# Cross-attention with layer norm on one core: the order of all engines' work written anew, with sums left in PSUM, copies moved between engines and low parts last

## The chip, the cores and the metric

The kernel runs on one core of one Trainium2 chip. The metric is the device time of one execution in microseconds (us). TensorE does the matrix products, VectorE and ScalarE work on SBUF and PSUM, GpSimd on SBUF, and SyncE starts most transfers. In the profile they are called PE (with PEld for the loads of weights), DVE, ACT, POOL and SP.

## The reference

```
qs  = (x @ wq)   per head (16 heads of 32), x: 4 x 2048 x 512, float32
ks, vs = (ctx @ wk), (ctx @ wv) per head, ctx: 4 x 77 x 512
scores = einsum('bhqd,bhkd->bhqk', qs, ks) / sqrt(32)
scores = where(mask, -inf, scores)
attn   = softmax(scores) @ vs
out    = attn @ wo + x
return (out - mean(out)) / sqrt(var(out) + 1e-5) * gamma + beta
```

## The kernel before

The 8192 rows of x are 64 tiles of 128 rows. Tiles t = 0 to 63 go in pairs (b = t // 2) and in groups of four (g = t // 4). To keep float32 accuracy, a large matrix is split into a high part and a low part (what the high part lost), both read by TensorE at full rate, and a product is high x high + high x low + low x high: 12 matmuls of 512 columns for 4 chunks c of the contraction.

A word of the table `ORDER` is one step; the first letter says what, the number which tile, pair or group. Each engine executes its own steps in the order of the table, and waits for the others through semaphores. The steps that matter here:

- `Qk` (L275, q_rows; 12 large matmuls into one PSUM bank, pq) makes a quarter of the queries of a group, `qk` (L289) copies it from PSUM to SBUF on VectorE. `i` and `j` (L265 on ScalarE, L269 on GpSimd) make the high part xth and the low part xtl of x.
- `St` (L405; 64 small matmuls into four banks, sc) makes a tile's scores. `Tt.part` (L422, VectorE) adds the mask, moves them to SBUF (pbuf) and takes the maxima of four heads, `et.part` (L437, ScalarE) the exponentials of four heads, `r` (L447, VectorE) the reciprocals of the sums, `n` (L452, GpSimd) the normalisation, `t` (L473, VectorE) a transpose, `Pb.n` (L484) one of twelve transfers that regroup a pair's transposed tiles into PT; the letter behind the number is the issuing queue (s SyncE, a ScalarE, g GpSimd).
- `Vb` (L498; 32 small matmuls into two banks, pa) multiplies a pair's PT with the values. `ab.i` (L527, ScalarE) takes the high part AH out of PSUM, `bb.i` (L531, VectorE) the low part AL.
- `Ot` (L554, o_proj; 12 large matmuls into one bank, po) is the output product of a tile. `+t` (L563, VectorE) adds the rows of x and writes the sum to SBUF (o), which frees the bank. `st` (L577, L578, VectorE) takes mean and variance, `vb` (L583 to L586, four small GpSimd steps) the factor and the shift of a pair (rn), `kt` (L592, ScalarE) scales, `ft` and `)t` (L595, L598, GpSimd) apply gamma and beta, `wt` (L601) stores.
- The last eight tiles, 56 to 63, go another way: `&` (L566) adds in PSUM, `s` or `~` takes the moments from PSUM, `u` (L618, L619, GpSimd) makes the factor, `y` and `z` (L634, L637, VectorE) finish.

There are eight PSUM banks; the table SLOTS["mm"] says which bank each product gets. A product can begin when the step that empties its bank's last user is done.

227 steps of the table stand on TensorE. Between two kinds of step (large, scores, values) TensorE changes the shape of its matmuls.

Of the kernel before, what the change touches and what calls it, by code (L numbers as in the profile page):

```python
# [8 lines left out]
F32 = mybir.dt.float32  # L9
# [25 lines left out]
for b in range(4):  # L35
# [7 lines left out]
NPB = 3  # L43
KSCALE = 1.0 / HD**0.5
# [30 lines left out]
T22.0 +12 T22.3 k10 k11 r20 n20 T22.2 T22.1 P9.0s O13 +13 P9.7s P9.11s e22.0 g17 s13 e21.2 e22.1 e21.0 P9.8s Z12.s
e21.3 P9.3s s12 v6 j15 b7.1 e22.2 Q26 x14 q26 t20 Q27 q27 r21 n21 S23 T23.3 T23.0 T23.1 g16 P9.1s e22.3 r22 V8 a8.1
b8.1 k13 e23.0 x15 a8.0 f4 t21 e23.3 e23.1 T23.2 e23.2 S24 T24.2 e24.2 T24.1 )4 b8.0 Q29 i17 n22 T24.3 f10 i16 )10 q29
T24.0 t22 f13 )13 e24.0 O14 +14 r23 e24.1 s14 S25 T25.0 T25.3 e25.3 n23 j16 T25.1 x16 O16 +16 e25.1 O15 +15 t23 s15 v7
O17 S26 T26.3 j17 e24.3 k15 T26.0 T25.2 P10.8s P10.4s r24 n24 V9 P10.7s P10.2s T26.1 k14 P10.0s w10 P10.6s P10.5s w13
P10.9s x17 P10.11s w4 +17 P10.1s P10.10s a9.1 b9.1 P10.3s e26.3 P11.5s s17 a9.0 e25.2 e25.0 T26.2 P11.3s P11.8s P11.7s  # L80
P11.1s P11.4s s16 v8 e26.0 k17 b9.0 f15 x19 P11.10s P11.2s Q28 q28 Q31 q31 g18 r25 n25 t24 P11.11s k12 g19 f17 k16 f16
)15 Q30 e26.1 q30 S27 T27.2 T27.3 T27.1 e27.2 V10 T27.0 e27.0 x18 e26.2 a10.1 t25 S28 T28.1 T28.2 f11 )11 r26 n26
P11.6s T28.0 P11.0s )17 P11.9s T28.3 w15 O19 +19 a10.0 b10.0 t26 P12.8s P12.0s P12.9s P12.3s w11 Q33 e27.3 P12.2s
P12.5s e28.1 e27.1 r27 f14 n27 b10.1 i19 i18 P12.7s O18 +18 s18 S29 T29.0 s19 v9 e28.2 w17 V11 a11.1 a11.0 T29.3 e28.3
b11.0 x23 P12.10s e28.0 k18 j18 t27 P12.4s x20 T29.2 e29.2 P12.1s O20 +20 O21 P13.8s P12.11s P13.5s P13.1s P12.6s
T29.1 P13.3s e29.1 e29.3 )14 w14 P13.2s s20 S30 j19 )16 T30.1 b11.1 T30.0 r28 n28 T30.3 e29.0 r29 e30.1 e30.0 k19
# [12 lines left out]
P17.0s f26 Q41 q41 n37 e38.2 P17.10s P17.8s P17.4s k27 w23 x31 k28 Q42 q42 S39 T39.2 P17.5s w25 T39.1 T39.3 e38.3 f27
k29 i24 P17.11s V16 a16.0 t37 j24 e39.3 r38 b16.0 n38 x30 P17.3s P17.9s S40 T40.3 T40.1 T39.0 e40.3 e39.1 P18.10s  # L100
P18.11s P18.8s P18.3s x32 P18.2s )26 P18.1s P18.6s P18.9s x33 O30 +30 s30 T40.0 O31 +31 t38 Q47 T40.2 a16.1 e39.0
e39.2 r39 n39 f28 s31 v15 b16.1 e40.2 e40.0 f29 )29 )28 S41 T41.3 e40.1 e41.3 T41.2 t39 V17 g25 T41.0 a17.1 T41.1
e41.2 L3 P18.4s P18.7s Q45 r40 w26 P18.5s b17.1 P18.0s P19.6s g27 n40 w28 P19.8s q47 Q44 q44 k31 f31 k30 f30 a17.0 i25
j25 S42 T42.1 P19.0s P19.1s P19.7s O33 e41.1 e41.0 )27 T42.0 T42.2 T42.3 e42.3 b17.0 O32 r41 +33 e42.0 s33 t40 S43 +32
e42.2 P19.9s P19.10s T43.2 P19.3s x34 w29 T43.0 P19.11s P19.2s T43.3 g26 x35 P19.5s P19.4s e42.1 T43.1 r42 n41 n42 s32
v16 t41 e43.3 V18 a18.0 a18.1 Q46 Q50 )31 =48.8 e43.1 e43.0 q46 q45 P20.5s i27 j27 P20.3s S44 P20.1s P20.9s x38 w27
q50 b18.0 P20.10s P20.7s T44.1 T44.0 x37 w31 T44.2 t42 O34 k33 T44.3 f33 e43.2 i26 k32 e44.0 e44.1 S45 T45.0 r43
# [67 lines left out]
def xattn_layernorm(  # L175
# [84 lines left out]
    def load_xT(g, c):  # L260
        fx[g, c] = buf([P, 2, GRP], F32, "xtf", name=f"xtf_{g}_{c}")
        nc.sync.dma_start(fx[g, c], xT[g, :, c : c + 2])
# [538 lines left out]
```

## Time and profile before

| what | value |
|---|---|
| time, median of 3 runs | 508.02 us (506.6, 508.02, 508.16) |
| span of the profiled execution, first to last instruction | 506.2 us |
| mean granted clock of TensorE | 0.998 |
| busy: PE, DVE, ACT, POOL | 498.8, 460.5, 473.9, 421.3 us |
| HBM read, written | 41.79 MB, 16.78 MB |

The profiled execution's own time is not listed apart from its span; the runs lie 0.4 to 2.0 us over it, for what is around the first and the last instruction. A group's row gives line, engine, operation, output and inputs, shape, count, busy time in us, the mean of one in ns, and the idle time ahead of it with what ended it. A timeline's row gives start, duration and the same names. In the busy line, PE counts matmuls whose ends are modelled and which overlap; the distance between two starts is what one costs.

### The profile page before, as it was taken

Reading aid. Unit: us, or ns where it says so; the run is one execution under the profiler, and the core shown is the slowest. Engines: PE = TensorE matmul, PEld = TensorE weight load, DVE = VectorE, ACT = ScalarE, POOL = GpSimd, SP = SyncE. Lnnn points to the kernel's source line nnn. Section 1 sums busy time; section 2 is a strip of 40 time slices with the busy share of each in tenths; the row PEclk is TensorE's granted clock in tenths of the full one; section 3 lists DMA queues with packets and bytes.
Section 4 is the critical chain, followed back from the end, with each engine's and each line's share of the span. In section 5 each row is a group of like instructions: output and inputs, shape, how many; then the busy total and the mean of one; then the engine's idle time right before and its main releaser. Section 6 shows DMA issues by size and latency. Waiting matters only on the chain.

```text
span 506.2 us, 20312 instructions
## 1 busy us (share of the span) xinstructions
PE 498.8 (99%) x6831; PEld 383.1 (76%) x6831; DVE 460.5 (91%) x2539; ACT 473.9 (94%) x2248; POOL 421.3 (83%) x387
## 2 busy tenths in 40 slices
PE   9999999999999999999999999999999999999995
PEld 6987778777777777777777777777777777877773
DVE  5799988999899999898898898998999999899997
ACT  6699999999999999999999999999999998999851
POOL 2666464789886798989989887999998999999896
PEclk9999999999999999999999999999999999999999
DMA  8957577889886796859887778877888769888746
GB/s 306 396 197 175 135 212 183 221 210 217 247 242 178 177 248 199 249 165 253 243 216 204 200 207 240 230 201 193 248 232 225 207 177 293 247 199 222 183 150 232
DMA packets 58782, 110.86 MB, mean 219 GB/s; under 512 B 9462, under 2 KB 11278, under 8 KB 58678
## 3 DMA queue, kind: packets, MB, share of 16 engines
q1 hardware_dynamic: 54502, 101.30, 71.1%
q0 software_dynamic: 2496, 5.77, 4.0%
q10 hardware_dynamic: 1680, 2.49, 2.0%
q8 instruction: 54, 0.88, 0.8%
q14 instruction: 50, 0.41, 0.3%
HBM read 41.79 MB, written 16.78 MB: 116 GB/s over the span
## 4 chain that ended last, share of the span: by engine, by line
PE 98%; DMA 1%; DVE 1%; ACT 0%; issue 0%; DVEq 0%
PE po L554 36%; PE pq L275 35%; PE pa L498 11%; PE sc L405 11%; PE pv L326 2%; PE pk L299 1%; PE pq L685 1%; DMA stage_a<-kin 1%; PE pa L513 0%; DVE xtl L637 0%; PE po L543 0%; DVE st L606 0%; DVE po L634 0%; ACT woh L672 0%; DVE mvt L608 0%
## 5 line engine op out<-in xcount | busy, mean ns | idle before, releaser
L437 ACT ACTIVATE pbuf<-pbuf,nm 128x77 f32<-128x77 f32 x1024 | 353.0, 358 | 5.2 <-DVE nm L422 3.6
L437 ACT ACTIVATION_READ_ACCUMULATOR pbuf<-pbuf,nm 128x1 f32 x1024 | 203.2, 198 | 0.0
L422 DVE CUSTOM_DVE_ANT_0 pbuf<-sc,mb 128x77 f32<-128x77 f32 x1024 | 169.7, 231 | 7.4 <-PE sc L405 5.8
L452 POOL TENSOR_TENSOR pbuf<-pbuf,ri 128x1232 f32<-128x1232 f32 x63 | 142.2, 2258 | 36.7 <-DVE ri L447 25.4
L554 PE MATMUL po<-woh,AH 128*128 128x512 f32 x256 | 103.5, 404 | 0.0
L473 DVE STREAM_TRANSPOSE B<-pbuf 128x1280 f32<-128x1280 f32 x64 | 96.1, 1502 | 5.8 <-POOL pbuf L452 2.4
L275 PE MATMUL pq<-xth,wqh 128*128 128x512 f32 (+1 forms) x256 | 100.8, 394 | 0.2
L554 PE MATMUL po<-wol,AH 128*128 128x512 f32 x256 | 99.9, 390 | 0.0
L554 PE MATMUL po<-woh,AL 128*128 128x512 f32 x256 | 99.8, 390 | 0.0
L275 PE MATMUL pq<-xth,wql 128*128 128x512 f32 (+1 forms) x256 | 98.1, 383 | 0.0
L275 PE MATMUL pq<-xtl,wqh 128*128 128x512 f32 (+1 forms) x256 | 98.1, 383 | 0.0
L422 DVE DVE_READ_ACCUMULATOR2_ANT nm<- 128x1 f32 x1024 | 84.4, 82 | 0.0
L598 POOL TENSOR_TENSOR o<-o,bet 128x512 f32<-128x512 f32 x56 | 72.1, 1291 | 1.8
L595 POOL TENSOR_TENSOR o<-o,gam 128x512 f32<-128x512 f32 x56 | 72.2, 1293 | 0.1
L269 POOL TENSOR_TENSOR xtl<-xtf,xth 128x1024 fp32r<-128x1024 f32 x28 | 67.2, 2404 | 3.9 <-ACT xth L265 3.2
L405 PEld LDWEIGHTS sc<-kct,q 32*64 32x64 f32 x4096 | 51.4, 130 | 22.6 <-issue 12.2
L405 PE MATMUL sc<-kct,q 32*64 32x77 f32 x4096 | 61.2, 238 | 0.0
L498 PE MATMUL pa<-PT,vsb 96*32 96x256 f32 x992 | 59.7, 382 | 0.0
L554 PEld LDWEIGHTS po<-woh,AH 128*128 128x128 f32 x256 | 48.0, 188 | 14.3 <-issue 2.5
L275 PEld LDWEIGHTS pq<-xth,wqh 128*128 128x128 f32 x256 | 48.1, 188 | 13.7 <-DVE nm L422 1.2
L554 PEld LDWEIGHTS po<-woh,AL 128*128 128x128 f32 x256 | 48.1, 188 | 10.5 <-DVE AL L531 0.2
L275 PEld LDWEIGHTS pq<-xth,wql 128*128 128x128 f32 x256 | 48.1, 188 | 9.7
(108 smaller groups left out, 638.6 us busy)
## 6 DMA issues: line engine op xcount, KB each, us to landing
PT<-B SPq DMA_DIRECT2D x330, 128.0 KB
xtf<-xT SPq DMA_DIRECT2D x28, 512.0 KB
o<-x SPq DMA_DIRECT2D x56, 256.0 KB
out<-o SPq DMA_DIRECT2D x56, 256.0 KB
PT<-B POOLq DMA_DIRECT2D x25, 128.0 KB, 4.0
PT<-B ACTq DMA_DIRECT2D x17, 128.0 KB
stage_a<-kin SPq DMA_DIRECT2D x4, 410.0 KB
xtf<-xT SPq DMA_DIRECT2D x4, 256.0 KB
```

Source lines behind the costliest of these rows:

```text
L269: return nc.gpsimd.tensor_tensor(l[:, c : c + 2], fx.pop((g, c)), xh[g][:, c : c + 2].bitcast(F32), ALU.subtract)
L275: nc.tensor.matmul(pq, w[:, c, m * P : (m + 1) * P], r[g][:, c, rs], start=(n == 0), stop=(n == 11))
L326: nc.tensor.matmul(pv[: rows.stop - rows.start], ctx_s[c][i][:, rows], v[c], start=(n == 0), stop=(n == 11))
L405: mm = nc.tensor.matmul(sc[j][r0 : r0 + SR, g * NK : (g + 1) * NK], qs[q, g, rs.start + r0 : rs.start + r0 + SR], kct[q, g, t // TPB, keys ...
L422: nc.vector.tensor_tensor_reduce(pb[:, h // 2, (h % 2) * NK : (h % 2 + 1) * NK], scs[t][j][:, g * NK : (g + 1) * NK], mb[:, t % TPB, keys_ ...
L437: nc.scalar.activation(pb[:, h // 2, (h % 2) * NK : (h % 2 + 1) * NK], pb[:, h // 2, (h % 2) * NK : (h % 2 + 1) * NK], AF.Exp, bias=nmax[t ...
L452: return nc.gpsimd.tensor_tensor(pv, pv, rv.to_broadcast((P, NP, 2, NK)), ALU.mult)
L473: nc.vector.transpose(bt.rearrange("p c q r -> p q c r"), pbuf[t % NPB].rearrange("p q (c r) -> p q c r", c=5),)
L498: nc.tensor.matmul(pas[b, g // 2][HD * j : HD * (j + 1), (g % 2) * BLK : (g % 2 + 1) * BLK], vsb[:, 2 * b // TPB, h % 2, HD * (h // 2) : H ...
L554: nc.tensor.matmul(pos[t], a[:, c, rs], w[:, c, :], start=(first and c == 0 and n == 0), stop=(c == NC_D - 1 and n == 2),)
L595: return nc.gpsimd.tensor_tensor(od[t], od[t], gam, ALU.mult)
L598: return nc.gpsimd.tensor_tensor(od[t], od[t], bet, ALU.add)
```

## The change

- The table of order is written anew for all engines, and with it the tables that give tiles their buffers and banks. TensorE changes its kind of step 145 times instead of 150.
- The matmuls of a q or output product stand in another order: the eight that take the high part of x or of the attention first, the four that take its low part last (`hi_then_lo`).
- A number behind `Q` or `O` puts so many empty instructions between the product's matmuls (`pad`): 445 in all, in 83 products.
- 13 tiles (2, 4, 22, 25, 28, 33, 34, 38, 39, 46 to 49; words `kt.2`) leave the sum with x in PSUM. The moments are taken from there, and VectorE instead of ScalarE subtracts the mean, multiplies with the factor and writes to SBUF, which frees the bank. Where both tiles of a pair do so, GpSimd leaves out the two steps that make the shift.
- 16 of the q copies (words `qk.1`) go to ScalarE.
- The new switches for loads by ScalarE's queue are used by no word. Each queue issues as many regrouping transfers as before.

The core of the diff; of the tables only the last line of `ORDER` is shown:

```diff
+def hi_then_lo(wh, wl, hi, lo):
+
+    return [(w, hi, c) for c in range(NC_D) for w in (wh, wl)] + [(wh, lo, c) for c in range(NC_D)]
...
-y62 O63 s63 )53 w53 z62 w62 u63 y63 z63 w63
+w60 z62 w62 )52 s63 u63 w52 y63 z63 w63
...
+CENTRED = {int(w[1:].split(".")[0]) for w in ORDER.split() if w[0] == "k" and "." in w}
+IN_PSUM = {int(w[1:].split(".")[0]) for w in ORDER.split() if w[0] == "k" and w.endswith(".2")}
...
-    def q_rows(pq, m, g, rs):
+    def pad(n, nops):
+        for _ in range((n + 1) * nops // 12 - n * nops // 12):
+            nc.tensor.nop(hint="pad")
+
+    def q_rows(pq, m, g, rs, nops=0):
         n = 0
-        for c in range(NC_D):
-            for w, r in ((wqh, xh), (wqh, xl), (wql, xh)):
-                nc.tensor.matmul(pq, w[:, c, m * P : (m + 1) * P], r[g][:, c, rs], start=(n == 0), stop=(n == 11))
-                n += 1
+        for w, r, c in hi_then_lo(wqh, wql, xh, xl):
+            nc.tensor.matmul(pq, w[:, c, m * P : (m + 1) * P], r[g][:, c, rs], start=(n == 0), stop=(n == 11))
+            pad(n, nops)
+            n += 1
...
-    def q_evac(g, m):
+    def q_evac(g, m, by_scalar=0):
         pq = qp.pop((g, m))
         if g:
-            nc.vector.tensor_copy(once(qd, g, [P, NG, GRP], F32, "q")[:, m, :], pq)
+            copy = nc.scalar.copy if by_scalar else nc.vector.tensor_copy
+            copy(once(qd, g, [P, NG, GRP], F32, "q")[:, m, :], pq)
...
-    def o_proj(t):
+    def o_proj(t, nops=0):
...
-        for c in range(NC_D):
-            for n, (a, w) in enumerate(((ah, woh), (ah, wol), (al, woh))):
-                nc.tensor.matmul(
...
+        for n, (w, a, c) in enumerate(hi_then_lo(woh, wol, ah, al)):
+            nc.tensor.matmul(pos[t], a[:, c, rs], w[:, c, :], start=(first and n == 0), stop=(n == 11))
+            pad(n, nops)
 
     def residual(t):
+        if t in IN_PSUM:
+            return residual_psum(t)
         nc.vector.tensor_tensor(od[t], pos.pop(t), od[t], ALU.add)
...
-        nc.vector.bn_stats(st, od[t])
+        nc.vector.bn_stats(st, pos.get(t, od[t]))
...
+        if not {2 * b, 2 * b + 1} <= CENTRED:
+            nc.gpsimd.tensor_tensor(rn[:, 1, :], mv[:, :, 0], rn[:, 0, :], ALU.mult)
+            nc.gpsimd.tensor_tensor(rn[:, 1, :], rn[:, 1, :], mneg, ALU.mult)
...
+        if t in CENTRED:
+            mean = mvs[t // 2][:, tt, 0:1]
+            return nc.vector.tensor_scalar(o, pos.pop(t, o), mean, rn[:, 0, tt : tt + 1], ALU.subtract, ALU.mult)
         nc.scalar.activation(o, o, AF.Identity, bias=rn[:, 1, tt : tt + 1], scale=rn[:, 0, tt : tt + 1])
```

Three places of the order, with the numbers of tiles in the names (a row of the order is line, operation, output and inputs, size; "x8" is eight equal instructions). TensorE's queue around the values product of pair 4 (pa_4), before:

```order
L405 MATMUL sc_15_1_2128<-kct_74,q_3_1140 64x77
L405 MATMUL sc_15_2_2129<-kct_74,q_3_1140 64x77
L405 MATMUL sc_15_3_2130<-kct_74,q_3_1140 64x77
L498 MATMUL pa_4_0_2179<-PT_4_1794,vsb_75 32x256 x8
L498 MATMUL pa_4_1_2180<-PT_4_1794,vsb_75 32x256 x8
L554 MATMUL po_5_2217<-woh_72,AH_2_1934 128x512
L554 MATMUL po_5_2217<-wol_73,AH_2_1934 128x512
L554 MATMUL po_5_2217<-woh_72,AL_2_1949 128x512
```

And now:

```order
L568 MATMUL po_6_1981<-wol_73,AH_3_1661 128x512
L568 MATMUL po_6_1981<-woh_72,AL_3_1724 128x512
L283 NO_OP
L568 MATMUL po_6_1981<-woh_72,AL_3_1724 128x512 x2
L283 NO_OP
L568 MATMUL po_6_1981<-woh_72,AL_3_1724 128x512
L283 NO_OP
L513 MATMUL pa_2_0_2040<-PT_2_1538,vsb_75 32x256 x8
L513 MATMUL pa_2_1_2041<-PT_2_1538,vsb_75 32x256 x8
L513 MATMUL pa_4_0_2072<-PT_4_1721,vsb_75 32x256 x8
L513 MATMUL pa_4_1_2073<-PT_4_1721,vsb_75 32x256 x8
L420 MATMUL sc_14_0_2107<-kct_74,q_3_1155 64x77
```

Two values products now stand side by side, ahead of the scores of tile 14 instead of behind those of 15; the product in front ends with its four low parts, and empty instructions lie between its matmuls.

VectorE's queue from the residual of tile 47 on, before (the residual L563 writes o in SBUF and frees po; st and mv are the moments, AL the low part of pair 24, ri a reciprocal, B a transposed pair):

```order
L563 TENSOR_TENSOR o_47_7390<-po_47_7707,o_47_7390 128x512
L531 TENSOR_TENSOR AL_24_7736<-pa_24_0_7643,AH_24_7661 128x512
L577 BN_STATS st_47_7751<-o_47_7390 128x6
L578 BN_AGGR mv_23_7753<-st_47_7751 128x2
L447 RECIPROCAL ri_55_7791<-sum_55_7605 128x16
```

And now (L577 writes po, L607 is the scale; in the places left out stand the maxima L437 of tile 56 and tile 57):

```order
L577 TENSOR_TENSOR po_47_8116<-po_47_8116,o_47_7986 128x512
...
L588 BN_STATS st_47_8188<-po_47_8116 128x6
L589 BN_AGGR mv_23_8173<-st_47_8188 128x2
L546 TENSOR_TENSOR AL_24_8180<-pa_24_0_8002,AH_24_8042 128x512
L304 COPY q_15_8192<-pq_15_1_8154 128x512
L488 STREAM_TRANSPOSE B_27_8200<-pbuf0_80 128x8x5x32
L462 RECIPROCAL ri_55_8268<-sum_55_8046 128x16
...
L607 TENSOR_SCALAR o_46_7908<-po_46_8101,mv_23_8173,rn_23_8274 128x512
...
L607 TENSOR_SCALAR o_47_7986<-po_47_8116,mv_23_8173,rn_23_8274 128x512
```

The bank of tile 47 was free after the first row; now it is free after the last, with two of VectorE's scales in between that wait for GpSimd's rn_23.

VectorE's last rows, before (st and mvt are the moments, L634 and L637 finish a tile into xtl):

```order
L606 BN_STATS st_63_9066<-po_63_9010 128x6
L608 BN_AGGR mvt_63_9068<-st_63_9066 128x2
L637 SCALAR_TENSOR_TENSOR xtl_15_7816<-po_62_9033,mvt_62_9049,bet_77 128x512
L634 SCALAR_TENSOR_TENSOR po_63_9010<-po_63_9010,mvt_63_9068,gam_76 128x512
L637 SCALAR_TENSOR_TENSOR xtl_15_7816<-po_63_9010,mvt_63_9068,bet_77 128x512
```

And now:

```order
L653 SCALAR_TENSOR_TENSOR xtl_15_8315<-po_62_9464,mvt_62_9499,bet_77 128x512
L622 BN_STATS st_63_9508<-po_63_9462 128x6
L624 BN_AGGR mvt_63_9510<-st_63_9508 128x2
L650 SCALAR_TENSOR_TENSOR po_63_9462<-po_63_9462,mvt_63_9510,gam_76 128x512
L653 SCALAR_TENSOR_TENSOR xtl_15_8315<-po_63_9462,mvt_63_9510,bet_77 128x512
```

The end of tile 62 stood behind the moments of tile 63 and now stands ahead of them.

More of the change, by code (lines that the diff above doesn't have):

```diff
@@ new lines @@
+e31.3 )17 P13.5s P13.10s T32.1 x23 x22 w18 e31.2 P14.1s P14.8s q36.1 r30 b12.1 O22.3 T32.0 P13.7s n30 P13.9s P14.10s
+b12.0 +23 P14.5s s23 x24 V13 S33 e32.2 P14.7s P14.9s r31 +22 t30 j21 s22 O24.16 T33.3 k20 P14.2s a13.0 a13.1 e32.0 w14
+P14.0s e32.1 P14.11s b13.1 T33.1 P14.4s e32.3 e33.1 w17 T33.0 v11 O25 Q39 k23 e33.0 g22 x25 k22.2 T33.2 n31 t31 P14.3s
+r32 +24 s24 +25 k21 S34 g23 s25 f20 e33.3 e33.2 P14.6s T34.3 T34.2 T34.1 P15.6s n32 P15.5s x27 b13.0 T34.0 Q38.4 V14
+f22 v12 f23 q39 e34.2 )22 i22 )23 e34.1 P15.10s a14.0 r33 q38 k25.2 S35 P15.9s P15.2s n33 t32 T35.0 P15.7s w19 T35.2
@@ new lines @@
+P17.7s b15.1 q41.1 t36 T39.2 T39.3 s29 f27 b15.0 w21 w25 Q46.8 P17.4s P17.5s P17.8s e38.1 P17.2s e38.0 e39.3 t37
+P17.10s q46.1 x31 O30.1 V16 P17.9s )27 T39.0 s28 P17.6s e39.0 w27 T39.1 S40 P17.0s +30 e39.2 O31.3 r38 a16.1 e39.1 s30
+T40.2 T40.1 P17.11s P18.7s P18.0s T40.3 r39 v14 n38 P18.3s T40.0 b16.1 a16.0 x32 +31 i24 )24 b16.0 w24 V17 j24 P18.6s
+k26 e40.1 x33 s31 k28.2 n39 S41 k29 i25 P18.4s P18.5s t38 f29 O33.2 P18.10s e40.3 f28 g27 T41.3 T41.2 )28 P18.11s
+T41.1 O32.9 T41.0 )29 a17.0 w28 P18.2s +33 b17.0 t39 S42 T42.0 Q47.2 e41.3 e40.2 v15 P18.1s e40.0 r40 w29 T42.2 T42.3
@@ new lines @@
+T42.1 P18.8s e41.0 e41.1 q47 P19.5s j25 P18.9s a17.1 e42.3 s33 P19.8s e42.0 +32 e41.2 x36 Q45.9 n40 x35 s32 f26 P19.1s
+t40 k30 e42.2 P19.10s e42.1 P19.2s b17.1 P19.9s q45.1 S43 v16 T43.0 Q44.4 P19.3s O35.2 )26 =48.8 T43.1 r41 T43.2 T43.3
+f30 n41 k32 i27 f32 )30 P19.7s V18 a18.1 r42 P19.11s P19.4s k33.2 P19.6s x37 +35 n42 q44 S44 a18.0 g26 t41 e43.1
+P20.7s j27 P19.0s Q50 b18.1 T44.3 w30 P20.10s P20.11s T44.1 e43.2 b18.0 P20.5s e43.3 T44.2 T44.0 w26 t42 P20.9s q50.1
+e43.0 S45 O37.5 i26 )32 r43 O36.1 P20.8s T45.2 e44.1 +37 e44.0 T45.0 T45.3 n43 O34.5 j26 +36 s37 k31 V19 g29 e44.3 f33
@@ new lines @@
+P25.11s P25.5s T55.3 x56 T55.2 T55.0 f45 e54.2 a24.1 t53 a24.0 e55.3 x53 P25.2s T55.1 e55.0 S56 f44 P26.4g O46.2
+O47.11 P26.5s T56.0 T56.2 r54 +46 P26.10g Q61.2 P26.0s P26.11s s46 )45 T56.3 b24.1 P26.9a +47 T56.1 s47 b24.0 q61 n54
+e56.2 t54 S57 O49.3 )43 e55.2 )44 e55.1 e56.1 r55 w45 x48 x59 v23 T57.3 P26.8g k46.2 T57.2 P26.6g n55 T57.1 P26.2a
+e56.3 e57.3 k47.2 e56.0 T57.0 P26.3s t55 x63 r56 e57.2 w43 V25 +49 e57.0 P27.0s P26.1s e57.1 P27.4a S58 Q63.9 T58.2
+T58.0 T58.3 f46 P26.7g O48.4 s49 )46 P27.8g P27.1g w46 r57 q63.1 a25.0 e58.0 a25.1 x54 P27.6s P27.9s T58.1 w44 S59
@@ new lines @@
+e61.2 b27.0 P28.3g b27.1 O55.3 P29.4g e62.0 T62.1 P29.2s P29.11a O54 e61.1 +53 +52 n60 v25 T62.3 P29.6s r61 x58 S63
+e62.1 T62.2 e62.3 x60 s52 s53 w48 n61 k50 e62.2 +55 V28 t60 v26 f50 T63.1 V29 k53 t61 P30.9s P30.6s r62 e63.1 P30.0s
+f53 a28.0 T63.0 n62 a28.1 T63.2 P30.2a P30.10s P30.1s P30.7s b28.1 b28.0 P30.5g P30.3g P30.4s a29.1 b29.1 e63.0 h63.0
+T63.3 O56 O57 s55 k52 t62 P30.11s )53 a29.0 e63.3 +54 P30.8s U62.2s U62.0s e63.2 U62.9s b29.0 U62.8a h63.1 &57 s54
+U62.1s O58 V30 ~57 )50 U62.3s w49 O59 m63.0 U62.4a U62.5g m63.1 &56 &58 t63 U63.1s v27 s56 U63.9a w50 U62.6s u57 s58
@@ L257, in xattn_layernorm, with load_xT @@
     pe_words = [w for w in ORDER.split() if w[0] in "HBQSVWXO"]
-    def load_xT(g, c):
+    def load_xT(g, c, by_scalar):
         fx[g, c] = buf([P, 2, GRP], F32, "xtf", name=f"xtf_{g}_{c}")
-        nc.sync.dma_start(fx[g, c], xT[g, :, c : c + 2])
+        (nc.scalar if by_scalar else nc.sync).dma_start(fx[g, c], xT[g, :, c : c + 2])
     def cast_xT(g, c):
@@ L538, in load_x @@
             od[t] = once(ends, t // 4, [P, 4, D], F32, "xth" if t < LAST + 4 else "xtl")[:, t % 4]
-        nc.sync.dma_start(od[t], x[t * P : (t + 1) * P, :])
+        (nc.scalar if by_scalar else nc.sync).dma_start(od[t], x[t * P : (t + 1) * P, :])
     def resid(t):
@@ L551, in o_proj @@
             pos[t] = bank(f"po_{t}")
-        for c in range(NC_D):
-            for n, (a, w) in enumerate(((ah, woh), (ah, wol), (al, woh))):
-                nc.tensor.matmul(
-                    pos[t],
-                    a[:, c, rs],
-                    w[:, c, :],
-                    start=(first and c == 0 and n == 0),
-                    stop=(c == NC_D - 1 and n == 2),
-                )
+        for n, (w, a, c) in enumerate(hi_then_lo(woh, wol, ah, al)):
+            nc.tensor.matmul(pos[t], a[:, c, rs], w[:, c, :], start=(first and n == 0), stop=(n == 11))
+            pad(n, nops)
     def residual(t):
+        if t in IN_PSUM:
+            return residual_psum(t)
         nc.vector.tensor_tensor(od[t], pos.pop(t), od[t], ALU.add)
@@ L739, in xattn_layernorm @@
             ins = ops[op](int(k or 0), int(part or 0))
-            if op in "FG":
+            if op in "FG" or op == "k" and k and int(k) in CENTRED - IN_PSUM:
                 shared = ins
-            elif shared and op in "jnf)":
-                wait_for(ins, shared, "VectorE's pass over two tiles of SBUF is begun ahead of GpSimd's")
+            elif shared and op in "jnf)v":
+                wait_for(ins, shared, "VectorE's pass over both of its ports is begun ahead of GpSimd's")
                 shared = None
```

200 lines of the change are left out of this document (88 added, 112 removed).

## The prediction

> **What bounds the kernel now.** I read the page's busy line and its chain first, then the busy time by stretch, then the single matmuls where TensorE goes from one kind of work to the next, and last the waits. The page's span, busy line and chain by engine, and the chain by line:
>
> ```profile
> span 506.2 us, 20312 instructions
> PE 498.8 (99%) x6831; PEld 383.1 (76%) x6831; DVE 460.5 (91%) x2539; ACT 473.9 (94%) x2248; POOL 421.3 (83%) x387
> PE 98%; DMA 1%; DVE 1%; ACT 0%; issue 0%; DVEq 0%
> ```
>
> ```profile
> by line: PE po L554 35.8%; PE pq L275 34.5%; PE pa L498 11.4%; PE sc L405 11.2%; PE pv L326 1.7%; PE pk L299 1.4%; PE pq L685 1.1%; DMA stage_a<-kin 0.7%; PE pa L513 0.4%; DVE xtl L637 0.3%; PE po L543 0.2%; DVE st L606 0.1%; DVE po L634 0.
> ```
>
> The end is set by TensorE from the first loads to the last output product. A busy TensorE could still be a slow one, so I looked at the long middle (stretch, length, busy time of PE, PEld, DVE, ACT and POOL, granted clock, DMA share, GB/s):
>
> ```profile
> 70.00:480.00 410.00, 409.99 (x5763) 312.41 (x5756) 379.89 (x2173) 404.15 (x1943) 362.20 (x319) 1.00 0.80 216
> ```
>
> Between 70 and 480 us TensorE has 0.01 us without a matmul, at the full granted clock (1.00). The kernel there is as long as its matmuls and what lies between two kinds of them. The timeline shows the price of a change of kind (start, duration; the distance of two starts is what a matmul costs):
>
> ```profile
> 264.01 0.39 PE L275 MATMUL pq<-xtl,wqh 128*128 128x512 f32 x1
> 264.24 0.39 PE L275 MATMUL pq<-xth,wql 128*128 128x512 f32 x1
> 264.56 0.95 PE L405 MATMUL sc<-kct,q 32*64 32x77 f32 x64
> 265.44 1.93 PE L498 MATMUL pa<-PT,vsb 96*32 96x256 f32 x32
> 267.30 0.95 PE L405 MATMUL sc<-kct,q 32*64 32x77 f32 x64
> 268.19 0.50 PE L554 MATMUL po<-woh,AH 128*128 128x512 f32 x1
> 268.53 0.40 PE L554 MATMUL po<-wol,AH 128*128 128x512 f32 x1
> ```
>
> A large matmul inside its stretch takes 0.23 us (264.01 to 264.24), the last before small ones 0.32, the first after small ones 0.34 (268.19 to 268.53). So each separate stretch of large matmuls costs 0.09 + 0.11 = 0.20 us on top. One tile's scores take 0.88 us, one values product 1.86, whatever follows.
>
> **The change, part by part.** *Fewer changes of kind, 150 to 145.* Counted in the two tables of order: stretches of large matmuls go from 58 to 57, neighbouring pairs of values products from 2 to 5, neighbouring pairs of scores from 2 to 3. What a pair is worth is in these rows:
>
> ```profile
> 68.67 3.66 PE L498 MATMUL pa<-PT,vsb 96*32 96x256 f32 x64
> 72.26 0.50 PE L554 MATMUL po<-woh,AH 128*128 128x512 f32 x1
> 20.86 1.76 PE L405 MATMUL sc<-kct,q 32*64 32x77 f32 x128
> 22.68 0.36 PE L275 MATMUL pq<-xth,wqh 128*128 128x256 f32 x1
> ```
>
> Two values products in a row take 3.59 us against 2 x 1.86 = 3.72, so a pair gains 0.13. Two scores in a row take 1.82 us against 1.76, so a pair loses 0.06. Sum: -0.20 - 3 x 0.13 + 0.06 = -0.53 us, all on the path. The five changes are a tenth of a per cent.
>
> *Low parts last.* The output product now asks for AL at its ninth matmul instead of its third, 6 x 0.23 = 1.4 us later, and q asks for the low part of x at its ninth instead of its second. That is worth what TensorE now waits for low parts (the waits: engine, line, for whom, us, times, longest; then the timeline):
>
> ```profile
> PEld po L554 <- DVE AL L531: 0.2, 1, 0.2
> ```
>
> ```profile
> 493.98 0.80 PE L554 MATMUL po<-woh,AH 128*128 128x512 f32 x1
> 494.62 0.40 PE L554 MATMUL po<-wol,AH 128*128 128x512 f32 x1
> ```
>
> There is one such wait in the run, and none for the low part of x. The first output product of the last pair takes 0.64 us to its second matmul where 0.34 is usual: I take -0.30 us, between 0 (the wait is for something else) and -0.41 (all over 0.23).
>
> *445 empty instructions on TensorE.* They lie between large matmuls, at most 21 in one product of 12. The trace of before holds none. From below: 0.88 us for the 64 matmuls and 64 weight loads of a tile's scores is 7 ns an instruction, so the queue has 0.23 us for every two instructions of a product and could take in two more unseen: cost 0. From above: if each kept the next weights from being loaded ahead, as behind a change of kind, 445 x 0.11 = 49 us. They also move the places where a new block of instructions begins, and could gain. Scores were stretched at a few places:
>
> ```profile
> 255.08 1.15 PE L405 MATMUL sc<-kct,q 32*64 32x77 f32 x64
> 256.16 0.50 PE L275 MATMUL pq<-xth,wqh 128*128 128x512 f32 x1
> ```
>
> Here a tile took 1.08 us instead of 0.88. In all, 11.2% of 506.2 is 56.7 us against 64 x 0.88 = 56.3, so at most 0.4 us is to be had. I take 0, since the row of the scores lies far nearer to it than the row of an unloaded weight. [...] No row here shows an empty instruction.
>
> *16 q on ScalarE, 13 scales on VectorE, 13 sums left in PSUM.* The durations (mean ns behind the comma):
>
> ```profile
> L289 DVE COPY q<-pq 128x512 f32<-128x512 f32 x60 | 40.0, 674 | 5.7 <-PE pq L275 5.7
> L592 ACT ACTIVATE o<-o,rn 128x512 f32<-128x512 f32 x56 | 44.2, 817 | 1.5 <-POOL mvt L619 1.2 <-POOL rn L586 0.3
> L527 ACT CAST AH<-pa 128x512 fp32r<-128x512 f32 x64 | 35.8, 580 | 4.5 <-PE pa L498 2.9 <-PE pa L513 0.7 <-ACT pbuf L437 0.4
> L563 DVE TENSOR_TENSOR o<-po,o 128x512 f32<-128x512 f32 x56 | 37.7, 676 | 1.8 <-PE po L554 1.7
> L566 DVE TENSOR_TENSOR po<-po,xth 128x512 f32<-128x512 f32 x4 | 2.7, 690 | 0.0
> L606 DVE BATCH_NORM_STATS2 st<-po 128x6 f32<-128x512 f32 x4 | 2.8, 699 | 0.2
> ```
>
> ScalarE: -13 x 0.817 + 16 x 0.580 (a copy out of PSUM like AH's) = -1.3 us. VectorE: -16 x 0.674 + 13 x 0.68 (a pass from PSUM, as the q copy; bounds 0.58 and 0.82) + 13 x 0.014 for a residual left in PSUM (0.690 against 0.676) = -1.8 us, the moments from PSUM (0.699) being much as long. GpSimd drops two of four small steps for three pairs of tiles. No engine but TensorE is the bound, so this is 0 on the path. What could cost is the bank: a sum in PSUM keeps its bank until VectorE has scaled it. The next user comes 8.4 us after the end of the product for tiles 2 and 47, 9 to 23 us for the other eleven (the large matmuls, 0.88, 1.86 and 0.20 added up along the new order). The tightest is tile 47. In VectorE's new queue there stand, from its residual to the end of its scale, 16 heads of maxima, six passes over a half thousand columns (residual, moments, AL, q, two scales), a transpose and two small ones. With the rows of a free-running VectorE:
>
> ```profile
> 440.24 0.23 DVE L422 CUSTOM_DVE_ANT_0 pbuf<-sc,mb 128x77 f32<-128x77 f32 x1
> 440.40 0.23 DVE L422 CUSTOM_DVE_ANT_0 pbuf<-sc,mb 128x77 f32<-128x77 f32 x1
> 441.03 0.69 DVE L289 COPY q<-pq 128x512 f32<-128x512 f32 x1
> 441.64 0.68 DVE L563 TENSOR_TENSOR o<-po,o 128x512 f32<-128x512 f32 x1
> 444.38 1.51 DVE L473 STREAM_TRANSPOSE B<-pbuf 128x1280 f32<-128x1280 f32 x1
> 445.81 1.25 DVE L289 COPY q<-pq 128x512 f32<-128x512 f32 x2
> ```
>
> 16 x 0.16 + 6 x 0.61 + 1.43 + two small steps of some 0.15 = 8.0 us, 0.4 under the 8.4: cost 0 if VectorE is on time. With whole durations (0.25 with its accumulator, 0.68, 1.51) it is 9.9, 1.5 too long. I take 0 and keep 1.5. The scale also adds a wait: VectorE now stands still until GpSimd's rsqrt of the pair is there, and behind it in its queue are the maxima that ScalarE's exponentials need.
>
> *The end.* VectorE now finishes tile 62 ahead of the moments of tile 63. Before:
>
> ```profile
> 499.54 0.55 POOL L619 TENSOR_TENSOR mvt<-mvt,small 128x1 f32<-128x1 f32 x1
> 500.07 0.70 DVE L606 BATCH_NORM_STATS2 st<-po 128x6 f32<-128x512 f32 x1
> 500.90 0.72 DVE L637 SCALAR_TENSOR_TENSOR xtl<-po,mvt,bet 128x512 f32<-128x512 f32 x1
> 501.54 0.75 DVE L634 SCALAR_TENSOR_TENSOR po<-po,mvt,gam 128x512 f32<-128x512 f32 x1
> ```
>
> The moments began as the last product ended. Now 0.64 us (500.90 to 501.54) of tile 62 stand in front, from 500.1 on, when GpSimd has its factor. The moments begin at 500.8, 0.7 late; of that some 0.4 was spent anyway behind them, while GpSimd worked on tile 63. I take +0.3 us, between 0 and 0.7.
>
> *All the rest of the order.* New waits of TensorE: 0 taken, since the old order of the same kind left it 0.01 us in 410. From the last q product to the first scores that need it the new order leaves 9.3 us in the median by the same adding up, the old one 5.5; from the scores of a pair's second tile to its values product it is 27.7 at the least against 29.0.
>
> **Sum:** -0.53 - 0.30 + 0.3 = -0.5 us on a span of 506.2. The three runs shown are 506.6, 508.02 and 508.16 us. The median lies 1.8 us over this span, and I keep that: 508.0 - 0.5 = 507.5 us. The runs differ by 0.3% among themselves, which is also about the least difference that can be told from none here, 1.5 us.
>
> **The rivals.** *A, the sum above.* For it speaks the full TensorE; against it, that it assumes that nothing new is late.
> *B, more of TensorE's small losses go than I count.* The 0.4 us of stretched scores, and what large matmuls lose beyond their own time and the edges. A piece of the chain without an edge gives that time:
>
> ```profile
> 85.71 5.44 PE pq L275 x24
> ```
>
> 0.2267 us each. The chain gives po, pq and pv 72.0% of 506.2 = 364.5 us; 1524 matmuls of 512 columns at 0.2267, 48 half as wide at half of it and 57 edges of 0.20 make 362.3. Some 2 us are lost here and there. Three quarters of the 2.4 in all: 507.5 - 1.8 = 505.7 us. For it speaks that empty instructions shift just these places; against it, that some gain and others lose when blocks move. It decides when a tile's scores never exceed 0.88.
> *C, slower: a bank comes free too late.* At tile 47, VectorE needs 8.0 us of work for 8.4. It comes late if it waits for GpSimd's factor:
>
> ```profile
> DVE o L563 <- PE po L554: 1.7, 4, 0.5
> ```
>
> ```profile
> L452 POOL TENSOR_TENSOR pbuf<-pbuf,ri 128x1232 f32<-128x1232 f32 x63 | 142.2, 2258 | 36.7 <-DVE ri L447 25.4 <-DVE nm L422 5.3 <-DVE wol L367 5.0
> ```
>
> VectorE waited for an output product 4 times in 56, so it usually starts behind TensorE already, and one normalisation of 2.26 us on GpSimd ahead of the factor is enough. The 1.5 us from above at this place and at one more of the 13: 507.5 + 3.0 = 510.5 us. It decides from 0.4 us of lateness at tile 47, from 2.4 at tile 46.
> *D, empty instructions are not free.* A tenth of the 49 us: 512 us.
>
> **How the numbers follow.** A 0.52, B 0.26, C 0.17, D 0.05. A alone spans 506.2 to 508.8 with the scatter of the runs. The range, 505.4 to 510.3, takes in B and most of C. Faster is B and the low edge of A: 0.29. Slower is C and D: 0.22. The same is what remains of A: 0.49.
>
> **What would show it.** Right: about 57 distances of 0.32 and 0.34 at the stretches' edges, pairs of values products at 3.59, 410 us of TensorE as full as before, the wait for AL gone, the last scale 0.3 us later after the last matmul. Wrong: TensorE idle ahead of the scores of tile 58 or of other users of held banks (C), large matmuls of over 0.23 us beside empty instructions (D), a chain in which ScalarE or VectorE holds more than 2%.

## The result and the profile after

| | before | after |
|---|---|---|
| time, median | 507.87 us (506.6 to 508.16) | 521.21 us (516.53 to 523.54) |
| ratio, 95% interval | | 1.0255 (1.0206 to 1.0304): slower |
| span of the profiled execution | 506.2 us | 514.7 us (its time is 516.53) |
| granted clock of the runs (of before the profiled one) | 0.998 | 0.998 (profiled), 0.989, 0.993, 0.986 |

The change costs 13.3 us in the median. The profile is of the fastest run; it shows 8.5 us of the loss. The page of after: span and busy line, the chain by engine, then the long middle (columns as before).

```profile
span 514.7 us, 20781 instructions
PE 501.1 (97%) x6831; PEld 385.1 (75%) x6831; DVE 459.8 (89%) x2536; ACT 473.3 (92%) x2251; POOL 419.6 (82%) x381
PE 70%; DVE 10%; DMA 7%; POOL 4%; SPq 4%; ACT 3%; issue 2%; POOLq 0%; DVEq 0%; ACTq 0%
```

```profile
70.00:480.00 410.00, 405.19 (x5732) 308.55 (x5724) 371.06 (x2142) 395.91 (x1915) 353.39 (x307) 1.00 0.78 212
```

TensorE has the same 6831 matmuls as before, and VectorE, ScalarE and GpSimd are no busier. But TensorE, 0.01 us short of full before, stands for 4.81 of 410 us, and 30% of the chain runs outside it, through VectorE, transfers, GpSimd and other queues. What TensorE waited for, largest first:

```profile
PE po L568 <- DVE o L574: 1.3, 2, 1.0
PE pa L513 <- DVE nm L437: 1.2, 1, 1.2
PE sc L420 <- DVE nm L437: 0.9, 4, 0.3
PE pa L513 <- DMA PT<-B: 0.8, 1, 0.8
```

These are small and of several kinds. The list misses waits inside a stretch of matmuls, so I also took, for each step of TensorE behind 66 us, the distance to the next step's start less the usual one (12 x 0.2267 us with the edges for a product, 0.88 for scores, 1.86 for values). Steps more than 0.1 us late lose 0.6 us in 2 places before and 10.3 us in 19 places after: O2 ahead of V3 0.5, V5 ahead of V6 1.4, S24 to S27 (182 to 216 us) 4.2, S54 to S56 1.2, V29 and O58 1.4 us, and so on. All steps together are 8.9 us later than before (11.2 against 2.3); less 0.5 us for fewer changes of kind, which this count leaves out, and with 0.2 us more at the end that is 8.6 us, and the spans differ by 8.5.

The longest single wait is V6 behind V5: what was counted as a pair worth 0.13 us costs 1.2, for a bank that VectorE's maxima had not emptied.

```profile
140.50 0.95 PE L420 MATMUL sc<-kct,q 32*64 32x77 f32 x64
141.38 1.93 PE L513 MATMUL pa<-PT,vsb 96*32 96x256 f32 x32
144.49 1.93 PE L513 MATMUL pa<-PT,vsb 96*32 96x256 f32 x32 [1.17 <-DVE nm L437]
```

### The profile page after: what moved, and what is told of

It is laid out like the page before. It is cut to its first block, busy times and chain, and to the rows that moved or that the text cites. A ratio compares the mean times of both kernels' runs of the same rounds, so it can differ in the third digit from the quotient of the medians.

```text
span 514.7 us, 20781 instructions
## 1 busy us (share of the span) xinstructions
PE 501.1 (97%) x6831; PEld 385.1 (75%) x6831; DVE 459.8 (89%) x2536; ACT 473.3 (92%) x2251; POOL 419.6 (82%) x381
## 4 chain that ended last, share of the span: by engine, by line
PE 70%; DVE 10%; DMA 7%; POOL 4%; SPq 4%; ACT 3%; issue 2%; POOLq 0%; DVEq 0%; ACTq 0%
PE pq L288 26%; PE po L568 25%; PE sc L420 8%; PE pa L513 8%; DMA PT<-B 4%; DVE pbuf L437 3%; SPq L499 2%; DVE B L488 2%; ACT pbuf L452 2%; POOL pbuf L467 2%; PE pv L341 2%; DMA xtf<-xT 1%; DMA m<-mask 1%; PE pq L701 1%; DMA stage_a<-kin 1%
## 5 line engine op out<-in xcount | busy, mean ns | idle before, releaser
L452 ACT ACTIVATION_READ_ACCUMULATOR pbuf<-pbuf,nm 128x1 f32 x1024 | 198.7, 194 | 0.0
L437 DVE CUSTOM_DVE_ANT_0 pbuf<-sc,mb 128x77 f32<-128x77 f32 x1024 | 170.6, 232 | 9.1 <-PE sc L420 6.4
L437 DVE DVE_READ_ACCUMULATOR2_ANT nm<- 128x1 f32 x1024 | 84.7, 83 | 0.1
L420 PEld LDWEIGHTS sc<-kct,q 32*64 32x64 f32 x4096 | 52.7, 130 | 25.1 <-issue 15.3
L568 PE MATMUL po<-woh,AL 128*128 128x512 f32 x256 | 68.4, 389 | 0.0
L288 PE MATMUL pq<-xtl,wqh 128*128 128x512 f32 (+1 forms) x256 | 66.7, 382 | 0.0
L420 PE MATMUL sc<-kct,q 32*64 32x77 f32 x4096 | 63.2, 238 | 1.3 <-DVE nm L437 0.9
L568 PEld LDWEIGHTS po<-wol,AH 128*128 128x128 f32 x256 | 48.1, 188 | 9.3 <-issue 0.2
```

The source lines that it names most:

```text
L288: nc.tensor.matmul(pq, w[:, c, m * P : (m + 1) * P], r[g][:, c, rs], start=(n == 0), stop=(n == 11))
L420: mm = nc.tensor.matmul(sc[j][r0 : r0 + SR, g * NK : (g + 1) * NK], qs[q, g, rs.start + r0 : rs.start + r0 + SR], kct[q, g, t // TPB, keys ...
L437: nc.vector.tensor_tensor_reduce(pb[:, h // 2, (h % 2) * NK : (h % 2 + 1) * NK], scs[t][j][:, g * NK : (g + 1) * NK], mb[:, t % TPB, keys_ ...
L452: nc.scalar.activation(pb[:, h // 2, (h % 2) * NK : (h % 2 + 1) * NK], pb[:, h // 2, (h % 2) * NK : (h % 2 + 1) * NK], AF.Exp, bias=nmax[t ...
L568: nc.tensor.matmul(pos[t], a[:, c, rs], w[:, c, :], start=(first and n == 0), stop=(n == 11))
```

## The experiments

The theory I began with (theory 1) was that the new order asks for transferred data, PT above all, before SyncE's queue has brought it. Rivals: the held banks and VectorE's scales (theory 2); the copies on ScalarE or the empty instructions (theory 3); later, that the cause lies with the computing engines and not with SyncE's queue (theory 2 of the later runs), above all with an engine that has too little slack (2a ScalarE, 2b VectorE).

**Which part of the change.** The order alone: the new tables, with all four extras out.

```diff
-Q10.3 ... q26.1 ... k22.2
+Q10 ... q26 ... k22
-    return [(w, hi, c) for c in range(NC_D) for w in (wh, wl)] + [(wh, lo, c) for c in range(NC_D)]
+    return [(w, a, c) for c in range(NC_D) for w, a in ((wh, hi), (wh, lo), (wl, hi))]
```

> The changed kernel's order and slots, but with the old order inside a product, no empty instructions, no q copy on ScalarE and no sum left in PSUM (all scales on ScalarE, residuals to SBUF). Theory 1, the order itself sets transfers later than TensorE and VectorE now ask for them: 517 to 523 us, 1.02 to 1.03 of before, with the same kind of small stalls (some 12 us in all). Theory 2, the held banks and the scales on VectorE: 507 to 509 us. Theory 3, the empty instructions or the q copies on ScalarE: also 507 to 509 us.

522.61 us, ratio 1.0268 (1.0227 to 1.0309): the order alone (with its tables of buffers and banks, which no run takes apart from it) is enough for all of it. Then the change without the sums in PSUM (`k22.2` to `k22`, all 13), and without the copies on ScalarE (`q26.1` to `q26`, all 16):

> The changed kernel, but the 13 sums go to SBUF and ScalarE scales them. Theory 1: 517 to 523 us, as the changed kernel (1.02 to 1.03). Theory 2: 507 to 510 us. Theory 3: as the changed kernel.

> The changed kernel with all q copies on VectorE. Theory 1: 516 to 524 us, as the changed kernel. Theory 3 (the copies on ScalarE, which now wait behind exponentials, hold up TensorE's banks and scores): 508 to 512 us.

The first takes 524.73 us in the median of the three runs that its ratio is worked out from (1.0317, 1.026 to 1.0374; a fourth took 532.44), the second 523.38 us in one run: neither part carries the loss. The old tables under the new code, first with low parts last alone, then with all empty instructions and ScalarE's copies (`Q7` to `Q7.4`, `q26` to `q26.1`):

> The old order and slots with nothing but the low parts last inside each product. By the prediction's term -0.3 us; by the profile after, where the last stall of TensorE (0.41 us ahead of an output product near the end) is still there, 0.0: 507.5 to 508.2 us, not to be told from before (0.997 to 1.003). If low parts last were itself the cost, 517 or more.

> The old order and slots with low parts last, the 445 empty instructions in the same 83 products and the 16 q copies on ScalarE. Theory 1 and theory 2: 507 to 509 us (0.997 to 1.003). Theory 3: 512 us or more.

507.85 us, 0.9988 (0.9973 to 1.0003): low parts last can't be told from nothing. But 527.32 us with the other two, 1.0344 (1.0286 to 1.0403): on the old order they cost 19 us. The waits say which:

```profile
PE sc L418 <- ACT q L302: 3.6, 2, 1.9
PE pa L511 <- ACT q L302: 2.4, 1, 2.4
PE sc L418 <- issue: 1.8, 1, 1.8
PE po L566 <- ACT q L302: 1.7, 1, 1.7
PE pq L286 <- issue: 1.2, 1, 1.2
```

7.7 us are for q copies that ScalarE reaches late, behind its exponentials; 3.0 us are put down to nothing. So the empty instructions alone, and once more for a second profile:

> The old order with low parts last and the 445 empty instructions alone; the 16 q copies stay on VectorE. If the 19 us of the run with both came from ScalarE's copies, for which TensorE waited 7.7 us there: 507 to 509 us (0.997 to 1.003). If the empty instructions cost: 515 us or more.

> The old order with the 445 empty instructions once more, for a profile: the runs lay between 508.7 and 515.4 us and the profiled one was the fastest. If the loss is in TensorE's instructions coming late, waits of 1 us and more that the profile puts down to nothing stand beside a block of instructions that lands late; if empty instructions take time of their own, large matmuls beside them lie over 0.24 us apart.

511.6 us, 1.009 (1.006 to 1.0119), runs from 508.7 to 515.4, and 509.91 us. They take no time of their own (in after, O17 with 18 of them has its matmuls 0.22 to 0.24 us apart behind the first), but the second profile shows TensorE standing in the middle of product Q60, where no semaphore is due:

```profile
429.77 0.50 PE L286 MATMUL pq<-xth,wqh 128*128 128x512 f32 x1
430.11 0.39 PE L286 MATMUL pq<-xth,wql 128*128 128x512 f32 x1
432.24 0.50 PE L286 MATMUL pq<-xth,wqh 128*128 128x512 f32 x1 [1.74 <-issue]
```

TensorE's instructions come in packets of 16 KB: the page's row of the queue (packets, MB, share) is `q8 instruction: 54, 0.88, 0.8%` before and `q8 instruction: 56, 0.92, 0.8%` in after, whose trace has 445 more rows of TensorE and at most 16 more of any other engine. The one due here began at 429.8 us, 11.7 us behind its forerunner, and took 0.95 us. In the faster profile of the same kernel it began at 428.5 and Q60 lost 0.6 us instead of 2.1; with low parts last alone, where the packets begin elsewhere, Q60 lost none. Scores, values and scores just ahead of Q60 use up 320 instructions in 3.6 us. So a late packet is the likely reason for this one wait; it is argued from two profiles. The longer runs of this kernel, up to 515.4 us, have no profile, and their granted clock is lower (0.991 and 0.992 in the two longest), so what the median loses is explained in part only.

**SyncE's queue.** In after SyncE waits 21.2 us, in 11 waits, to load x where a store of the same buffer has not landed (before 3.3 us):

```profile
SPq L554 <- DMA out<-o: 21.2, 11, 4.9
```

A ninth buffer takes these waits away; and on the old order the loads of x were put as early as in the new one:

```diff
-    "o": "765401234567217460721563402710625340671532607453071436270612457",
+    "o": "765401234567218746082153476802756134278061524730624870512604583",
```

> The changed kernel with a ninth buffer for the rows of x (o): the buffer loaded anew is then the one stored longest ago, 7 to 32 of SyncE's transfers earlier (median 17) instead of 1 to 23 (median 8). To make room, the identity matrix is built late in a dead buffer. Theory 1 in this form (SyncE stands 21.2 us, in 11 waits, ahead of loads of x for a store of the same buffer, and the regrouping transfers queued behind come late): those waits fall under 5 us, the stalls of TensorE by half or more, 508 to 513 us. If these waits are harmless and something else in the order makes the values late: 517 to 523 us, as the changed kernel.

> The old order with low parts last, but the loads of x stand earlier in SyncE's queue, so that a buffer is loaded 1 to 22 transfers after its store (median 8, as in the new order) instead of 3 to 27 (median 12). Theory 1 in this form: SyncE's wait for stores goes from 3.3 us to 15 or more, and the time to 511 to 520 us. Otherwise 507 to 509 us.

522.94 us, 1.0311 (1.0241 to 1.0381), with no such wait left in the middle; and 508.6 us, 1.0016 (1.0003 to 1.0029), though SyncE waits 18.7 us for stores there, in 10 waits. This form of theory 1 is out. The next form: a pair's twelve regrouping transfers stand too far apart, with 5 to 16 others between.

```diff
-P4.1s P2.0s ... P5.6s P6.8s P5.10s
+all parts of one pair ahead of the next pair's, in the same places
```

> The changed kernel; among the places that SyncE's regrouping transfers of pairs 4 to 30 have in the order, all of one pair come ahead of the next pair's (64 of them change places), so that 3 to 9 instead of 5 to 16 other transfers stand between a pair's first and last (2 to 10 in the old order). Theory 1, in the form that a pair's twelve transfers are spread too far (they take 16.3 us where the old order takes 12.6) and so its PT and its B buffer come late: 508 to 514 us and a mean time of 13 us for the twelve. Theory 2, that the cause is not in SyncE's queue: 517 to 524 us.

The twelve now take 12.6 us, as before, instead of 16.3, and the values products start 10.2 us behind the end of their last issue instead of 7.7 (before 11.2; means of pairs 4 to 21). Yet 519.08 us, 1.0246 (1.0187 to 1.0305). The theory had its means and not its effect. Two larger rewritings of SyncE's queue, which turned out to test something else:

> The changed kernel with SyncE's queue written anew from the trace: at each place the transfer that is ready and whose reader stands first; the other engines keep their order. A pair's twelve transfers then stand together (0 to 4 others between them). Theory 1: 506 to 512 us. Theory 2, that the cause is in the order of the computing engines: 516 us or more, though the values' parts land earlier.

> The old order with low parts last on all computing engines, but SyncE's queue in the new order (38 of 532 transfers had to come forward, since their readers would wait for ever). Theory 1: 513 to 524 us. Theory 2: 507 to 510 us.

656.99 us (1.2921, 1.287 to 1.2973) and 693.71 us (1.3617, 1.3499 to 1.3736). In both SyncE stood behind transfers that could not begin yet: 129.3 us ahead of loads of x whose buffer GpSimd's low parts still read in the first, 127.6 us ahead of stores whose rows GpSimd had not finished in the second. They show only what a queue costs whose order does not agree with that of the other engines.

**Which engine lacks slack.** The changed kernel with work taken from one engine at a time:

```diff
-        nc.scalar.activation(o, o, AF.Identity, ...)                    # less_scalar
-        nc.vector.bn_stats(st, pos.get(t, od[t]))
+        nc.vector.bn_stats(st, pos.get(t, od[t])[:, :64])               # less_vector
-        "f": lambda k, part: gain(k)
+        "f": lambda k, part: None                                       # less_gpsimd
-        nc.sync.dma_start(out[t * P : (t + 1) * P, :], od.pop(t))
+        nc.sync.dma_start(out[t * P : t * P + 16, :], od.pop(t)[:16])   # less_stores
```

> The changed kernel without ScalarE's 43 scales (left out: rows are not multiplied with the factor), 34.4 us of its 473.3. In the profile before ScalarE is busy 404.2 of 410 us in the long middle, TensorE 410.0: ScalarE is a second bound, and a wait of more than some 6 us on it can't be made good. Theory 2a (ScalarE's lack of slack turns each small delay of the new order into a delay of the end): 506 to 511 us. Theory 1 (transfers) and theory 2b (VectorE's queue, which empties PSUM banks late): 516 us or more.

> The changed kernel with the moments of 56 tiles taken of 64 columns instead of 512 (left out: the other columns), some 25 to 35 us less of VectorE's 459.8. Theory 2b (VectorE, in order and 89% busy, empties banks late): 506 to 511 us. Theories 1 and 2a: 516 us or more.

> The changed kernel without GpSimd's 56 multiplications with gamma (left out), 71.9 us of its 419.6. If GpSimd's lateness (the transposes wait for its normalisations, stores for its last step) is what the new order can't take: 506 to 511 us. Theories 1, 2a and 2b: 515 us or more.

> The changed kernel, but each store writes 16 of the 128 rows of its tile (left out: the others), so that 14.7 of the 110.9 MB that are moved fall away, while SyncE issues as many transfers as before. Theory 1, in the form that the transfers land late because the queues are loaded: 506 to 512 us. Theories 2a and 2b: 516 us or more.

ScalarE 520.32 us, 1.0258 (1.0225 to 1.0292); VectorE 515.72, 1.0153 (1.0128 to 1.0177); GpSimd 521.65, 1.0276 (1.0226 to 1.0326); stores 515.11, 1.015 (1.012 to 1.018). ScalarE, 98.6% busy in the middle before (404.15 of 410), is not what holds the new order back, nor is GpSimd: 27.6 us less of ScalarE's busy time and 69.7 us less of GpSimd's bring nothing. VectorE's load and the stores bear on it, each for 5 to 6 us, and neither brings the old time.

**The places.** Four values products moved back behind the steps that follow them in the new order:

```diff
-V3 a3.0 ... O0.1        V4 ... S14        V6 ... S19 ... O8        V30 ... O59
+O0.1 V3 a3.0 ...        S14 V4 ...        S19 ... O8 V6 ...        O59 V30 ...
```

> The changed kernel with four values products moved back on TensorE, each with its two copies: V3 behind O0 (3.8 us later), V4 behind S14 (0.9), V6 behind S19 and O8 (3.7), V30 behind O59 (2.8). In the changed kernel TensorE lost 0.5, 0.2, 1.4 and 0.9 us in the steps at these places, in five other runs of the new order up to 3.6, 1.7, 1.4 and 1.5 us. Theory 1 (the new order asks for PT before its transfers have landed): the waits at these four places fall under 0.3 us, the rest stays, 513 to 518 us. Theory 2b (VectorE empties banks late): the same loss turns up at the next bank, 516 us or more.

> The same four moves, with the moments of 64 columns and stores of 16 rows (left out: the rest of both). If the three reliefs add up (6.1 for the stores, 5.5 for VectorE, 2 to 4 for the places): 508 to 511 us, and TensorE's waits under 3 us. If something not yet named holds the new order back: 513 us or more.

521.14 us, 1.0249 (1.0197 to 1.03), and 522.25 us, 1.0284 (1.0258 to 1.031). At O2, V5 and O58 the waits went from 0.5, 1.4 and 0.9 us to 0.0. But V3 and V30 now lost 1.1 and 1.3 us at their new places, S19, the step behind the old place of V6, 1.3, and S14 2.6. The three reliefs do not add up: with all of them the time is that of the changed kernel. (The two reliefs together without the moved products were not run.) What this looks like, in the last kernel at S54 (VectorE, TensorE and GpSimd in turn):

```profile
409.98 1.51 DVE L523 STREAM_TRANSPOSE B<-pbuf 128x1280 f32<-128x1280 f32 x1 [0.55 <-POOL pbuf L502]
411.42 1.25 DVE L609 TENSOR_TENSOR o<-po,o 128x512 f32<-128x512 f32 x2
```

```profile
409.49 0.34 PE L455 MATMUL sc<-kct,q 32*64 32x77 f32 x2 [0.16 <-DVE q L339]
412.12 1.37 PE L455 MATMUL sc<-kct,q 32*64 32x77 f32 x58 [2.30 <-DVE o L609]
```

```profile
407.70 2.25 POOL L502 TENSOR_TENSOR pbuf<-pbuf,ri 128x1232 f32<-128x1232 f32 x1 [3.52 <-DVE ri L497]
```

S54 needs the bank that the residual of an output product frees. On VectorE that residual stands behind the transpose t51, t51 waits for GpSimd's normalisation, and ahead of that GpSimd had stood idle for 3.52 us, until VectorE's reciprocals were there. TensorE stood 2.3 us.

One row tells the two orders apart in every profile: VectorE's transposes, with the idle time ahead of them behind the bar. Before, after, and the order alone:

```profile
L473 DVE STREAM_TRANSPOSE B<-pbuf 128x1280 f32<-128x1280 f32 x64 | 96.1, 1502 | 5.8 <-POOL pbuf L452 2.4 <-POOL o L595 1.4 <-DMA PT<-B 1.0
```

```profile
L488 DVE STREAM_TRANSPOSE B<-pbuf 128x1280 f32<-128x1280 f32 x64 | 96.2, 1505 | 11.9 <-DMA PT<-B 4.6 <-POOL pbuf L467 2.4 <-issue 1.8
```

```profile
L488 DVE STREAM_TRANSPOSE B<-pbuf 128x1280 f32<-128x1280 f32 x64 | 96.1, 1503 | 15.7 <-POOL pbuf L467 8.8 <-DMA PT<-B 2.4 <-DMA xtf<-xT 2.1
```

It is 4.7 to 7.4 us in the six profiles with the old order on all computing engines and SyncE's near it, 10.7 to 22.7 us in the twelve with the new order on the computing engines, sp_by_need aside. This row marks the order and not the loss: the old order with empty instructions and q copies has 4.7 us at 527 us, and less_vector, one of the two fastest with the new order, has 20.6 us. Products that began under 0.3 us after their bank was emptied (70 to 480 us) are 11 before, 22 after and 25 with the order alone, but 10 with the ninth buffer, whose profile spans 524.7 us. So neither count measures the cause, and no run changed either by itself.

**What is settled.** Shown: the new order with its tables is enough for the whole loss, and the extras add nothing to it, though two of them cost 19 us on the old order; it isn't the buffers of x, the spread of the regrouping, ScalarE's or GpSimd's load; where the four products were moved, other waits came. Likely, and only argued: the new order lets VectorE's queue stand in front of transposes with bank-freeing passes behind. For it speaks that of the 4.3 us of waits that the view lists for TensorE between 70 and 480 us in after, 3.7 end with a VectorE pass, and with the order alone 5.6 of 6.5 us. Left open: which of its differences would have to be undone. No single one that I tried was enough.

## Why the prediction was wrong

The prediction was 507.5 us, 505.4 to 510.3, with slower at 0.22. Point by point:

- *What bounds the kernel:* right, TensorE at 409.99 of 410 us. I took it as a proof of reserve. It says only that nothing was late with the old order.
- *Fewer changes of kind, -0.53 us:* the price list holds. In after a pair of values products takes 3.59 us where nothing is late, the first large matmul after small ones 0.34 (72.22 to 72.56); inside a stretch a large matmul takes 0.23 us, with a high part (75.30 to 75.53) as with a low part (74.17 to 75.08 for four):

```profile
68.63 3.66 PE L513 MATMUL pa<-PT,vsb 96*32 96x256 f32 x64
72.22 0.50 PE L288 MATMUL pq<-xth,wqh 128*128 128x512 f32 x1
72.56 0.39 PE L288 MATMUL pq<-xth,wql 128*128 128x512 f32 x1
```

- *Low parts last, -0.30 us:* 0. The wait ahead of O62 is 0.4 us in after and in the old order with low parts last, as before, so it wasn't for the low part's place; the run of this part alone stays within what can be told from no change.
- *445 empty instructions, 0:* mis-sized. They cost 3.7 us on the old order, neither by their own time nor by unloaded weights (49 us), but, as it seems, through instruction packets that come late, seen in one product. I had named moved blocks as a gain or a loss of 0.4 us at most. Of the 56 packets one shows in that second profile, by 1.74 us of waiting in one product; no other wait of TensorE there is put down to nothing.
- *16 q on ScalarE, 13 scales on VectorE, banks held, 0:* the work falls as said, but by less than half as much (ACT 473.9 to 473.3, DVE 460.5 to 459.8 us, against -1.3 and -1.8). Rival C's place was wrong: S58 lost 0.13 us, and without held banks the kernel is no faster. That copies on ScalarE are free is true of the new order only; in the old one they are, by difference, the larger part of 19 us (no run has them alone).
- *The end, +0.3 us:* right: from the start of the last matmul to the end 6.55 us before, 6.79 after.
- *All the rest of the order, new waits 0:* **this is the step that failed.** It was taken from the old order's success and from two leads added up along the new one (9.3 us from q to scores; 27.7 us from scores to values against 29.0). In its place there are 8.9 us of waits in the fastest run; the median loses 13.3 us. The leads that I added up were TensorE's own. Most of the waits that came end with VectorE's passes, which empty the banks, and for VectorE's queue I added up nothing but tile 47's bank. Why VectorE comes late stays open. The 12 regrouping transfers, too, had 8.6 others between them instead of 5.6 (mean of pairs 4 to 21), which could be counted in the table beforehand; but putting them together again did not bring the time back. The sign that I had named, a chain with more than 2% of ScalarE or VectorE, came: VectorE holds 10%, ScalarE 3%. The range of this term was worse than its value: an order of 2100 words written anew got no uncertainty at all.
- *Scatter of the runs:* not foreseen. See the last section.

## What to carry to other kernels

A full TensorE (409.99 of 410 us) was no reserve here: with the computing engines busy for 83 to 99% of the span, a new order of the same work brought 8.9 us of waits at its handovers. So before trusting a new order count, on each queue, what stands between producer and consumer, and give "no new waits" a range from the number of handovers. A wait that is taken away at its place can turn up at another step, as it did here with the four products that were moved; test reliefs together before adding them up. A change that mixes an order with switches should be run in parts: here one part is free only in the order it was made for.

## What the runs showed of the hardware

*Some gaps cost twice.* In 18 places of the profiles (the two kernels of 657 and 694 us aside) TensorE's granted clock fell to 0.50 for 3.41 us, once for 6.83, and large matmuls lay 0.43 us apart. In the 3.41 us ahead of each, TensorE had been idle for 0.8 to 2.5 us in sum. That gives no sharp threshold: 1.74 us in Q60 above and 1.83 us in less_stores (86.3 to 89.7 us) were not followed by a fall. All 18 begin a whole number of 3.413 us after the clock first stood at 1.00: in before and after, where it fell only behind the last matmul, it had stood at 1.00 for 498.35 and 508.59 us, 146 and 149 times 3.413, and the two falls of order alone begin 197.98 us apart, at 199.11 and 397.09, which is 58.0 times. Order alone, 198 to 204 us, the clock being third from the end; then its timeline:

```profile
198.00:200.00 2.00, 1.74 (x61) 1.43 (x62) 1.93 (x5) 2.00 (x13) 2.00 (x3) 0.78 0.21 73
200.00:202.00 2.00, 2.00 (x6) 1.52 (x6) 1.86 (x7) 2.00 (x13) 1.84 (x4) 0.50 0.04 8
202.00:204.00 2.00, 2.00 (x9) 1.65 (x8) 0.49 (x6) 1.43 (x7) 1.92 (x4) 0.87 0.59 145
```

```profile
200.21 0.63 PE L288 MATMUL pq<-xtl,wqh 128*128 128x512 f32 x1
200.64 0.63 PE L288 MATMUL pq<-xth,wql 128*128 128x512 f32 x1
...
203.12 0.40 PE L288 MATMUL pq<-xth,wqh 128*128 128x512 f32 x1
203.35 0.39 PE L288 MATMUL pq<-xtl,wqh 128*128 128x512 f32 x1
```

Each such stretch loses 3.41 x 0.5 = 1.71 us; the profiles have 0 to 3 of them (after none, order alone 2, old order with empty instructions and q 3). A mean clock of 0.986 to 0.993 against 0.998 is, by an estimate from these figures, 1.5 to 3.6 of them, 2.6 to 6.2 us. The other three runs of after are 4.4 to 7.0 us longer than the profiled one, so the clock has the size of this scatter; but it does not order the runs, for the longest lost the least by it.

*Instructions came late*, as it seems, to TensorE behind many small ones (320 in 3.6 us): 1.7 us in one place, in the kernel where 445 instructions that do nothing had moved the packets' borders.
